# Reciprocals and norm pieces of a cross attention queued on VectorE behind the last instruction written in their step

## The chip, the cores and the metric

The kernel runs on one core of one Trainium2 chip: TensorE (PE), VectorE (DVE), ScalarE (ACT), GpSimd (POOL) and the DMA queues of SyncE (SP). The metric is the device time of one execution in microseconds (us), lower is better. Times are medians over several runs; the profile shows a single execution.

## The reference

One decoder layer in float32 on x of 16 sequences x 112 tokens x 512 features, with a context of 16 x 375 x 512: a self attention, a masked cross attention and a feed-forward block, each on a normalised x and each added to x. Of it the cross attention matters here:

```python
q = proj(hs, Wq, bq)            # 16 heads of 32
k, v = proj(at, Wk, bk), proj(at, Wv, bv)
scores = einsum('bhsd,bhtd->bhst', q, k) / sqrt(32)
scores = clip(where(attend, clip(scores, -50, 50), -10000), -50, 50)
probs = softmax(scores)
probs = probs / (probs.sum(-1) + 1e-8)
ctx = einsum('bhst,bhtd->bhsd', probs, v)
delta = clip(residual_scale, 0, 0.3) * (ctx @ Wo.T + bo)
delta = (delta - mean) / sqrt(var + 1e-5) * gamma + beta
x = x + delta                   # then layernorm(x) goes into the feed-forward block
```

## The kernel before

The program runs three stages: self attention (to about 330 us of the span), cross attention (to about 821 us) and the feed-forward block (to the end). The order of TensorE's instructions is the order in which the program is written, by hand. The other engines' orders are made by a scheduler when the kernel is built: among the instructions that its own clock holds ready for an engine it takes the one written first. Each engine then works through its queue in that order, whatever the chip's timing is.

**Steps.** The cross attention goes through 16 batches b and, in each, three thirds kc of the 375 context rows. `cross.step(b, kc, ...)` is one step, called (b,kc) here. In the timeline a step begins with the scores, TensorE's L929. It writes, in this order:

1. the scores of this third into two PSUM tiles "sc", and their exponentials on ScalarE (L1330) into tiles e or es;
2. for the third before: the weighted values (`weigh`, L940), the additions that sum its exponentials into the batch's es (`add`, VectorE, L1367; only for kc over 0), and at the end of a batch `divide`: the key sums on TensorE (L951), their copy into r on ScalarE (L1376), the copy of the unnormalised output into xyT (L1378), and a generator `quotients`, kept in `self.parts`;
3. the Relu check of the scores on ScalarE (L1338), which gives the score banks free;
4. `f.fill(us)`: filler work for TensorE, about us long, mostly keys and values of the next batch. Its products go into the three banks of the tag "mm" in turn, and VectorE reads each one out (the bank reads L907, L1019, L1023, L1035, L1076, L1078). Queries are read out by ScalarE (L892);
5. for b > 0 and kc > 0, pieces of `self.parts`.

`quotients` has four pieces, each a reciprocal of a quarter of r (L1383) and a product into xyT (L1384), and at its end a Relu on ScalarE (L1386). Two pieces are taken in the step with kc 1 and the rest with kc 2. As `divide` for batch b-1 is written in step (b,0), the pieces in (b,1) and (b,2) belong to batch b-1. Where b is a multiple of 4, step (b,0) takes all four at once and without any tie (L1346); the last batch's are taken after the loop.

**Norm pieces.** The main loop takes pieces of a generator `finish` in the steps with kc > 0 of batches that are not the first of their group of four: 3 in each step of an odd place in the group, 2 in an even one (L1818). At batch 1 they are the norm before the cross attention for the last group (`Norm.steps`: an rstd chain of 12 tiny instructions, L784 to L796, then one L802 for each of 4 tiles). At batches 5 and 9 they are `AfterCross.finish` for a whole group of tokens: one chain, then for each of 3 or 4 tiles two products and the statistics (L1291, L1299, L776, L777), then `Norm.steps` of the next norm.

**The ties.** Both kinds of piece stand in a `tc.issue_after(ins)`. It puts what is written inside it on the engine of `ins` (VectorE here) behind `ins` in that engine's queue: an order of issue, without a wait for the end of `ins`. ScalarE's instructions inside are not tied. Before, `ins` is `cross.last`, the addition L1367 that was written last. In a step with kc 1 no addition is written, so `cross.last` is there an addition of the step before. And an addition is written one step later than its exponentials, but its place in VectorE's queue is where these are ready, one step earlier:

```profile
494.22 1.14 PE L929 MATMUL sc<-q,kT 32*125 32x112 f32 x32
...
501.90 1.54 DVE L1383 RECIPROCAL r<-r 128x112 f32<-128x112 f32 x2
...
507.42 1.14 PE L929 MATMUL sc<-q,kT 32*125 32x112 f32 x32
...
518.13 1.14 PE L929 MATMUL sc<-q,kT 32*125 32x112 f32 x32
```

These are rows of the timeline (start, length, engine, line): steps (5,0), (5,1) and (5,2) begin at 494.22, 507.42 and 518.13. The two reciprocals at 501.90 are written in (5,1) and run in (5,0).

Of the kernel before, what the change touches and what calls it, by code (L numbers as in the profile page):

```python
# [584 lines left out]
def mixed(a, b, skip=0):  # L585

    a, b = iter(a), iter(b)
    for _ in range(skip):
        yield next(a)
    while True:  # L590
        took = [next(p, None) for p in (a, b)]
        if took[0] is None and took[1] is None:
            return
        yield sum(t for t in took if t is not None)
# [3 lines left out]
def finite_layer(  # L598
# [30 lines left out]
    nc = tc.nc  # L629
# [22 lines left out]
    def pair(name, tag="e", bufs=3):  # L652
        return evp.tile([P, 2, HG, S], F32, tag=tag, name=name, bufs=bufs)
# [267 lines left out]
    def scores(k_of, q_of, rows_):  # L921

        scs = [psum("sc", [P, 2, 512]) for _ in range(2)]
        views = [
            s[:rows_, :, : HG * S].rearrange("p i (j s) -> p i j s", j=HG) for s in scs
        ]
        for j in range(C):
            for i in range(HG):
                nc.tensor.matmul(  # L929
                    views[i // 2][:, i % 2, j, :], k_of(i, j), q_of(i, j), start=True, stop=True  # L930
                )
        return views
# [171 lines left out]
    def after_self(tiles, norm):  # L1104

        for t in tiles:
            yield from project(
                wo, t, lambda acc: nc.vector.tensor_tensor(xr[:, t, :], acc, xr[:, t, :], ALU.add)
            )
            stats(xr[:, t, :], norm.l, t)  # L1110

    class SelfAttention:
# [35 lines left out]
        def step(self, b, grp, f, us, prepared):  # L1148
            b, v, es = self.next
            if b + 1 < B:  # L1150
                self.begin(b + 1, grp)
            with tc.issue_after(self.behind.ins):
                for _ in range(prepared):
                    next(w2_prep, None)
            first = max(0.45 * us, min(us, 5.5))
            f.fill(first)
            eTs = []
            for e, share in zip(es, (0.45 * (us - first), 0.35 * (us - first))):
                tr = psum("sc", [P, 2, 512])
                trv = tr[:S, :, : HG * S].rearrange("p i (j s) -> p i j s", j=HG)  # L1160
                for i in range(2):
                    for j in range(C):
                        nc.tensor.transpose(trv[:, i, j, :], e[:, i, j, :], ident[:S, :S])  # L1163
                eT = pair("eT")
                nc.scalar.copy(eT[:S], trv)
                eTs.append(eT)
                f.fill(share)
            y = psum("ys", [P, C, S])
            weighted_values(y, v[b % GB][:S], eTs, True, True)
            nc.scalar.copy(xyT[:, :, ts(b, S)], y)  # L1170
            f.drain()
# [96 lines left out]
    class AfterCross:  # L1268
# [15 lines left out]
        def finish(self):  # L1284
# [23 lines left out]
                yield 0.0  # L1308
            yield from self.norm.steps()

    class Cross:


# [4 lines left out]
        def step(self, b, kc, q, keys, f, us):  # L1318
            scs = scores(
                lambda i, j: keys.third(keys.k[ds(i * DH, DH), j], kc),  # L1320
                lambda i, j: q[ds(i * DH, DH), j, ts(b % 2, S)],
                KP,
            )
            n = b * KC + kc
            late = self.late

            es = [(pair("es", "es", 3) if kc == 0 else pair("e"))[:KP] for _ in scs]
            self.late = (b, kc, keys.v[kc][:KP], es)
            for i, sc in enumerate(scs):
                nc.scalar.activation(  # L1330
                    es[i], sc, AF.Exp, scale=scl[:, n : n + 1], bias=bia[:, n : n + 1]
                )
            self.weigh(late)
            for i in range(2):
                self.add(late, i)
            self.divide(late)
            for i, sc in enumerate(scs):
                nc.scalar.activation(  # L1338
                    sc,
                    sc,  # L1340
                    AF.Relu,
                    scale=nscl[:, n : n + 1],
                    bias=limit[:KP, :1],
                    accum_out=low[:KP, 2 * n + i : 2 * n + i + 1],
                )
            if kc == 0 and b % GB == 0:  # L1346
                for _ in self.parts:
                    pass
            f.fill(us)
            if b > 0 and kc > 0:  # L1350
                with tc.issue_after(self.last):
                    for _ in range(2 if kc == 1 else C):
                        next(self.parts, None)

# [49 lines left out]
    def load_blocks(u, i):  # L1404

        o = block_tile("f")
        for half in range(2):
            nc.sync.dma_start(
                out=o[:, ds(2 * half, 2)].rearrange("p s k m -> p (s k) m"),
                in_=f_w[i][:, ts(u + UNITS * half, P)].rearrange("(c p) m -> p c m", p=P),  # L1410
            )
        behind = tc.issue_after(done[-2]) if len(done) > 1 else nullcontext()
        with behind:
            s_sums(o[:, 4:], *(o[:, k] for k in range(4)))
        return o
# [359 lines left out]
    cross = Cross()  # L1775
# [3 lines left out]
    for b in range(B):  # L1779
        g, bl = divmod(b, GB)  # L1780
        us = 0.0
        if b + 2 < B:
            kv.append(Keys(b + 2))
        if b + 1 < B:
            kv[b + 1].sums()
            us += 19.5
        if bl == 0:
            if g == 0:
                f.add(after_self(whole[3], n2[3]))
                finish = n2[3].steps()  # L1790
            elif g < 3:
                c = AfterCross(whole[g - 1], n3[g - 1])
                f.add(c.projections())
                finish = c.finish()
            us += 13.0 if g < 3 else 0.0
        if b + 1 < B:


            f.add(kv[b + 1].pieces())
            if b % 2:  # L1800
                queries = qs[(b + 1) // 2].pieces()
                us += 6.0
                if bl == 3 and g < 3:
                    n = n2[3] if g == 0 else n3[g - 1]
                    queries = mixed(queries, n.transposes(), 6)
                    us += 2.0
                f.add(queries)
        if b == B - 1:
            after = [AfterCross(whole[g], n3[g]) for g in (2, 3)]
            f.add(after[0].projections())  # L1810
            us += 10.5
        if b == B - 2:
            ready.update({(0, i): load_blocks(0, i) for i in range(2)})
        if b == B - 1:
            passes[0].token_sums()
        for kc in range(KC):
            cross.step(b, kc, qs[b // 2].q, kv[b], f, us / KC)
            if bl > 0 and kc > 0:  # L1818
                with tc.issue_after(cross.last):
                    for _ in range(2 + bl % 2):  # L1820
                        next(finish, None)
        f.drain()
# [100 lines left out]
@with_exitstack  # L1923
def decoder_layer(ctx: ExitStack, tc: tile.TileContext, *args):
    nc = tc.nc
    flag = ctx.enter_context(tc.tile_pool(name="flag", bufs=1))
    unfit = flag.tile([1, 1], I32, name="unfit")
    finite_layer(tc, unfit, *args)
    with tc.If(nc.values_load(unfit, min_val=0, max_val=1, skip_runtime_bounds_check_because="a comparison gives 0 or 1") > 0):
        general_layer(tc, *args)  # L1930
# [49 lines left out]
```

## Time and profile before

| | us |
|---|---|
| median of 3 runs (lowest, highest) | 1359.68 (1359.52, 1360.47) |
| the profiled execution | 1361.94 |
| its span, first to last instruction | 1360.2 |
| mean granted TensorE clock | 0.998 of full speed |
| TensorE busy in the span | 1338.4 (98%) |
| TensorE busy, 345 to 830 us | 482.29 of 485.00 |
| VectorE busy, 345 to 830 us | 327.19 of 485.00 |
| ScalarE busy, 345 to 830 us | 245.16 of 485.00 |
| L1383, reciprocals, 64 of them | 51.4 busy, 0.829 each |
| L1367, additions, 64 of them | 68.9 busy, 1.088 each |

How to read the profile: times are from the start of the span. A row of the timeline has the start, the length, the engine, the line of the kernel, the operation, out<-in with shapes and the number of instructions merged into it; in brackets stands how long the engine stood idle before it and whom it waited for. TensorE's float32 matmuls show as two records each, so x8 is four matmuls. Matmuls are pipelined and the ends of their records are modelled: the spacing of starts tells more than the lengths. A row of the table of windows has a stretch, its length, then the busy time of PE, PEld (weight loads), DVE, ACT and POOL with the number of instructions, the granted clock, the share of the DMA engines and GB/s.

### The profile page before, as it was taken

The page shows a single profiled execution, that of the slowest core. Times are in us where ns is not written, and L with a number is a line of the kernel's source. Part 1 is how long each engine was busy: PE and PEld are TensorE (multiplying, and loading weights), DVE is VectorE, ACT ScalarE, POOL GpSimd, SP SyncE. Part 2 cuts the span into 40 slices and gives each one's busy share as a digit, 9 for nine tenths or more (in the row PEclk, how much of TensorE's full clock was granted, in tenths as well). Part 3 has the DMA queues.
Part 4 walks back from the last instruction along what each step waited for, and adds up shares of the span by engine and source line. Part 5 has one row for each costly group of instructions (what it writes and reads, how often), then busy time and mean ns, then how long its engine had stood idle before and what let it go on. Part 6 is the DMA issues. An engine that isn't in the chain of part 4 may idle for free.

```text
span 1360.2 us, 20765 instructions
## 1 busy us (share of the span) xinstructions
PE 1338.4 (98%) x8508; PEld 840.2 (62%) x8508; DVE 820.0 (60%) x1666; ACT 476.9 (35%) x933; POOL 47.4 (3%) x72
## 2 busy tenths in 40 slices
PE   8999999999999999999999999999999999999997
PEld 5555555556788778868887874544555555555553
DVE  3267987873666577657765588557653245554332
ACT  2445664554445535454545553201110011111000
POOL 3000001040000100000000000000000000000000
PEclk9999999999999999999999999999999999999999
DMA  9100003711111111111121111111031112322201
GB/s 312 62 1 0 32 1 94 245 37 40 27 28 28 35 28 28 28 28 27 37 45 28 32 48 31 47 47 47 33 123 62 47 62 70 93 83 72 93 0 57
DMA packets 93579, 76.16 MB, mean 56 GB/s; under 512 B 44657, under 2 KB 81568, under 8 KB 91172
## 3 DMA queue, kind: packets, MB, share of 16 engines
q1 hardware_dynamic: 91744, 71.51, 17.3%
q0 software_dynamic: 736, 1.65, 0.4%
q8 instruction: 69, 1.13, 0.4%
q10 hardware_dynamic: 996, 1.59, 0.3%
q14 instruction: 34, 0.28, 0.1%
HBM read 63.72 MB, written 11.01 MB: 55 GB/s over the span
## 4 chain that ended last, share of the span: by engine, by line
PE 92%; DVE 5%; ACT 1%; issue 1%; DMA 1%; POOL 0%; DVEq 0%; ACTq 0%; POOLq 0%
PE gate L1547 12%; PE mm L884 10%; PE mm L1013 9%; PE mm L902 8%; PE ys L1547 7%; PE mm L913 7%; PE mm L1073 6%; PE gate L1481 6%; PE mm L1547 5%; PE sc L929 5%; PE ys L940 4%; PE ys L1481 4%; PE mm L1481 3%; PE sc L1163 2%; PE mm L845 1%; PE mm L951 1%
## 5 line engine op out<-in xcount | busy, mean ns | idle before, releaser
L1330 ACT ACTIVATE e<-sc,bia,scl 125x896 f32<-125x896 f32 x64 | 68.5, 1095 | 133.9 <-PE sc L929 133.9
L1338 ACT ACTIVATE sc<-sc,limit,nscl 125x896 f32<-125x896 f32 x96 | 103.2, 1075 | 0.0
L1367 DVE TENSOR_TENSOR es<-es,e 125x896 f32<-125x896 f32 x64 | 68.9, 1088 | 55.7 <-ACT e L1330 55.6
L1547 PE MATMUL gate<-t,f 128*128 128x448 f32 x256 | 101.4, 539 | 0.0
L1481 PE MATMUL gate<-h,f 128*128 128x448 f32 x224 | 86.6, 539 | 0.0
L1547 PE MATMUL gate<-xyT,f 128*128 128x448 f32 x192 | 80.1, 540 | 0.0
L1130 ACT ACTIVATE e<-sc,mx 112x112 f32<-112x112 f32 x256 | 64.6, 400 | 41.1 <-DVE mx L1126 41.1
L1383 DVE RECIPROCAL r<-r 128x112 f32<-128x112 f32 x64 | 51.4, 829 | 45.3 <-ACT r L1376 45.2
L1547 PEld LDWEIGHTS gate<-t,f 128*128 128x128 f32 x256 | 48.6, 190 | 47.6 <-issue 47.2
L1547 PE MATMUL ys<-t,f 128*128 128x448 f32 x192 | 77.4, 539 | 0.0
L1563 ACT COPY u<-gate 128x448 f32<-128x448 f32 x16 | 8.5, 532 | 183.5 <-PE gate L1547 110.5
L1481 PEld LDWEIGHTS gate<-h,f 128*128 128x128 f32 x224 | 42.5, 190 | 41.3 <-issue 40.9
L902 PE MATMUL mm<-xv,cT 128*125 128x512 f32 x144 | 66.3, 602 | 0.0
L1013 PE MATMUL mm<-kt,xks 128*128 128x188 f32 x360 | 65.1, 324 | 0.0
L1013 PEld LDWEIGHTS mm<-kt,xks 128*128 128x128 f32 x360 | 59.7, 190 | 2.9 <-issue 0.7
L1547 PEld LDWEIGHTS ys<-t,f 128*128 128x128 f32 x192 | 36.5, 190 | 35.7 <-issue 35.5
L902 PE MATMUL mm<-wv,xyT 128*112 128x512 f32 x128 | 58.0, 596 | 0.0
L1125 DVE TENSOR_REDUCE mx<-sc 112x8 f32<-112x896 f32 x32 | 33.5, 1084 | 40.6 <-PE sc L929 40.5
L1493 DVE TENSOR_TENSOR h<-h,h 128x896 f32<-128x896 f32 x32 | 32.8, 1085 | 40.9 <-PE ys L1481 31.7
L1547 PEld LDWEIGHTS gate<-xyT,f 128*128 128x128 f32 x192 | 36.0, 190 | 34.4 <-issue 33.0
L929 PEld LDWEIGHTS sc<-q,kT 32*125 32x125 f32 x1536 | 46.2, 183 | 15.3 <-issue 14.5
L929 PE MATMUL sc<-q,kT 32*125 32x112 f32 x1536 | 54.7, 279 | 0.0
(222 smaller groups left out, 2435.8 us busy)
## 6 DMA issues: line engine op xcount, KB each, us to landing
f<-in_f_w SPq DMA_DIRECT2D x64, 256.0 KB, 3.2
f<-blocks SPq DMA_DIRECT2D x14, 1024.0 KB, 4.8
cT<-in_ctx SPq DMA_DIRECT2D x32, 250.0 KB, 3.9
w<-in_f_w SPq DMA_DIRECT2D x4, 1024.0 KB, 10.3
blocks<-w SPq DMA_DIRECT2D x4, 1024.0 KB, 5.7
cT<-in_ctx SPq DMA_DIRECT2D x32, 126.0 KB, 3.5
xr<-in_x SPq DMA_DIRECT2D x2, 1024.0 KB, 10.7
out_y<-o SPq DMA_DIRECT2D x8, 256.0 KB, 3.2
```

The costliest lines, as they stand in the source:

```text
L884: nc.tensor.matmul(acc[:, :n], w[:, c, ts(j, P)], src[:, c, :], start=(c == 0), stop=(c == C - 1))
L902: nc.tensor.matmul(acc[:n, :], src[:, c, :], w[:, c, :], start=(c == 0), stop=(c == C - 1))
L913: nc.tensor.matmul(acc, xyT[:, c, ts(t, P)], w[:, c, :], start=(c == 0), stop=(c == C - 1))
L929: nc.tensor.matmul(views[i // 2][:, i % 2, j, :], k_of(i, j), q_of(i, j), start=True, stop=True)
L1013: nc.tensor.matmul(acc[:, m], w[:, k, ts(m, P)], x[:, k], start=k == 0, stop=k == 1)
L1073: nc.tensor.matmul(acc, x[:, k, :n], w[:, k], start=k == 0, stop=k == 1)
L1130: nc.scalar.activation(e[:, i, j, :], sc[:, i, j, :], AF.Exp, scale=SCALE, bias=mx[:, i, j : j + 1],)
L1330: nc.scalar.activation(es[i], sc, AF.Exp, scale=scl[:, n : n + 1], bias=bia[:, n : n + 1])
L1338: nc.scalar.activation(sc, sc, AF.Relu, scale=nscl[:, n : n + 1], bias=limit[:KP, :1], accum_out=low[:KP, 2 * n + i : 2 * n + i + 1],)
L1367: self.last = nc.vector.tensor_tensor(total, total, late[3][i][:KP], ALU.add).ins
L1481: nc.tensor.matmul(banks[m][bank], o[:, c, ts(m, P)], t[:, c, :], start=first and c == 0, stop=c == UNITS - 1, skip_group_check=True,)
L1547: nc.tensor.matmul(bank, o[:, s, k, :], t[:, k, :], start=first and k == 0, stop=k == 1, skip_group_check=True,)
```

## The change

A function `latest()` returns the VectorE instruction written last so far. Both ties now take it in place of `cross.last`. For the pieces of `self.parts` that is the last VectorE instruction of the step's filler, where the step has written any; for the norm pieces, which are taken after the step's call, it is the last product of `quotients` where the step has written one, else the same. What is computed, the instructions, and TensorE's order stay as they are.

```diff
+    def latest():
+
+        return next(
+            i
+            for i in reversed(nc.cur_bb.bb.instructions)
+            if i.engine == mybir.EngineType.DVE
+        )
+
     class Cross:
...
             f.fill(us)
             if b > 0 and kc > 0:
-                with tc.issue_after(self.last):
+                with tc.issue_after(latest()):
                     for _ in range(2 if kc == 1 else C):
                         next(self.parts, None)
...
         for kc in range(KC):
             cross.step(b, kc, qs[b // 2].q, kv[b], f, us / KC)
             if bl > 0 and kc > 0:
-                with tc.issue_after(cross.last):
+                with tc.issue_after(latest()):
                     for _ in range(2 + bl % 2):
                         next(finish, None)
```

## The prediction

> **What bounds the kernel now.** I read the page first, then who TensorE waited for in the cross attention (345 to 830 us), then the timeline around the longest of those waits, then the busy time of single steps. The page:
>
> ```profile
> PE 1338.4 (98%) x8508; PEld 840.2 (62%) x8508; DVE 820.0 (60%) x1666; ACT 476.9 (35%) x933; POOL 47.4 (3%) x72
> ...
> L1383 DVE RECIPROCAL r<-r 128x112 f32<-128x112 f32 x64 | 51.4, 829 | 45.3 <-ACT r L1376 45.2
> ```
>
> TensorE sets the time; VectorE matters only where TensorE has to wait for it. The reciprocals stand at the head of VectorE's queue for 45.2 us waiting for ScalarE's copy of the key sums, with the bank reads behind them. What that costs TensorE (line waited for: us, times, longest):
>
> ```profile
> PE mm L1073 <- DVE v L907: 2.4, 2, 1.4
> PE mm L884 <- DVE kT L1023: 0.3, 1, 0.3
> ```
>
> So there is little to win. By the starts of successive matmuls against their usual spacing the losses are 1.6 us at 502.5, 0.45 at 524.3 and 1.15 at 725.6: 3.2 in all, 0.24% of the run. The first, in the timeline (start, length, engine, line):
>
> ```profile
> 498.88 0.54 ACT L1376 COPY r<-mm 128x448 f32<-128x448 f32 x1
> ...
> 499.37 1.41 DVE L1299 SCALAR_TENSOR_TENSOR xr<-d,rstd,xr 128x512 f32<-128x512 f32 x2
> ...
> 501.34 1.44 PE L1013 MATMUL mm<-cT,xk 128*128 128x188 f32 x8
> 501.90 1.54 DVE L1383 RECIPROCAL r<-r 128x112 f32<-128x112 f32 x2
> ...
> 503.49 0.68 DVE L907 COPY v<-mm 125x512 f32<-125x512 f32 x1
> ...
> 504.22 1.13 PE L1073 MATMUL mm<-xv,cT 128*125 128x256 f32 x4 [1.44 <-DVE v L907]
> ```
>
> This is step (5,0) (batch 5, first third). Norm pieces and a pair of reciprocals, written for (5,1), run a step early, ahead of the first bank read L907. The bank is due when L1013 ends, at 502.6; the read ends at 504.1. That is the pattern by which I price the rest: the mm tile has three banks, so the read of one is due two products later.
>
> **What moves.** Now the pieces may start after an addition that VectorE did one step before; after the change, only behind the last VectorE instruction written in their own step, in practice a bank read. Nothing is added or removed: 48 of the 64 reciprocals move (batches 4, 8, 12 and the last finish theirs on a path the diff leaves alone), with all norm pieces. No DMA and no SP or POOL instruction is among them; the closing Relu (L1386, ScalarE) isn't tied but follows the last product. The durations, from one start to the next:
> - a pair of reciprocals with products: 806.93 to 808.72, 1.8 us;
> - one rstd chain: 520.40 to 523.72 less the addition inside, 2.3;
> - one tile of after-cross norm (L1291, L1299, statistics): 0.66 + 1.72 = 2.4, two interleaved 4.1;
> - two L802: 1.0.
>
> **Part 1, the gain.** (5,0) loses norm and reciprocals, so L907 is on time: -1.6. The 1.15 at 725.6 is batch 11's four reciprocals in (12,0), on the untouched path: it stays. At 524.3 L1023 will still have norm work before it: 0 (bounds -0.45 to +0.45).
>
> **Part 2, plain pairs.** Most steps get 1.8 us after their last bank read. TensorE then runs scores (1.14), weighted values (0.97) and two products before it needs a bank; the first bank read comes some 3.5 us after the scores began and can slip by two products less its own length, 1.27 + 0.86 - 0.5 = 1.6. Hidden, 0. If that cover went, each would cost up to 1.8.
>
> **Part 3, norm bursts.** Behind the last bank read of (5,1) now stand a pair, the chain and two tiles: 1.8 + 2.3 + 4.1 = 8.2; of (5,2) a pair, a tile, a chain, one L802: 1.8 + 2.4 + 2.3 + 0.5 = 7.0. For batch 9: 8.2, then a pair, two tiles and a chain, again 8.2. They land in steps with this much busy time (length; PE, PEld, DVE, ...):
>
> ```profile
> 518.13:528.19 10.06, 9.77 (x106) 8.87 (x105) 9.52 (x27) 5.48 (x9) 1.14 (x1) 1.00 0.40 92
> 528.19:537.54 9.35, 9.35 (x97) 6.07 (x96) 4.18 (x10) 5.56 (x9) 0.00 (x0) 1.00 0.01 2
> 648.61:658.15 9.54, 9.54 (x106) 8.86 (x105) 9.16 (x27) 5.48 (x9) 1.21 (x1) 1.00 0.42 96
> 658.15:667.50 9.35, 9.35 (x97) 6.08 (x96) 5.94 (x14) 5.56 (x9) 0.00 (x0) 1.00 0.01 3
> ```
>
> Step (5,2): of 9.5 VectorE us, 5.6 were norm work that leaves (1.7 of a tile, a chain, three L802); 3.9 + 8.2 = 12.1 in 10.06, so 2.0 spill into (6,0). There L907 is due by 536.6 (L1013 at 535.31 plus 1.27). If the spill and the whole second burst stand before it, it ends at 528.2 + 2.0 + 7.0 + 0.7 = 537.9: 1.3 late. If VectorE's order lets it in between the links of the chain, as bank reads were at 620 to 626, it costs 0. I take 0.7. Step (9,2): 6.8 leave (649.15 to 653.66 without an addition 3.5, a chain, two L802); 9.2 - 6.8 + 8.2 = 10.6 in 9.54, 1.1 spill; in (10,0) L907 is due at 666.5, and with 1.1 + 8.2, the key sums' differences (2.1 at 658.54) and itself it ends at 670.2: 3.7 late at worst, 0 at best. I take 2.0. Batch 1 has only 5.1 us (a pair, a chain, two L802) and 2.8 of such work; VectorE's free time there is 3.7 us in 389.51 to 399.01 and 5.8 in the step after: 0.
>
> **Part 4, additions pushed back.** The additions that the key sums need are written one step later than the pair, and of the work that is ready VectorE's queue has the earlier written first, as here the differences L1443. In (14,2), which also holds four token differences, the second addition was already last:
>
> ```profile
> 800.92 1.08 DVE L1443 TENSOR_TENSOR t<-xyT,t 128x896 f32<-128x896 f32 x1
> ...
> 801.92 0.72 DVE L1023 SCALAR_TENSOR_TENSOR kT<-mm,dbk,kT 128x188 f32<-128x188 f32 x2
> 802.57 1.08 DVE L1367 TENSOR_TENSOR es<-es,e 125x896 f32<-125x896 f32 x1
> ...
> 803.56 1.09 PE L951 MATMUL mm<-es,ones 125*32 125x448 f32 x8
> ```
>
> Its exponential was ready at 798.3, yet it ran at 802.57, and the key sums L951 (1.09, elsewhere 0.94) barely got it. VectorE has no free time in this step. It now gets a pair at its start (behind (14,1)) and one behind L1023, both ahead of that addition: 1.8 to 3.6 late; 0 if the order lets the addition in first. I take 2.7, nearer the order seen. (10,2) gets a pair and two L802 more and may hold back (11,0)'s key sums: 0 to 2.8, taken 0.5.
>
> **The sum.** -1.6 + 0 + 0 + 0.7 + 2.0 + 2.7 + 0.5 = +4.3 us. The profiled execution took 1361.94 us, its span 1360.2 with 1.7 around it, so it would become 1366.2. The median of the runs shown, 1359.68, is 2.26 below that execution; the same shift gives 1364.0, 0.32% slower.
>
> [...]
>
> **Rivals.**
> - A, no change (the other side): one mechanism, the place in VectorE's queue. If in (6,0), (10,0) and (15,0) the bank reads and the addition slip in before the moved work, only part 1 is left: 1359.68 - 1.6 = 1358.1. It decides once parts 3 and 4 come to under about 4.3 us. For it: reads were let in between chain links in step (9,0). Against: L907 was not, in (5,0), nor the addition in (14,2).
> - B, faster: the work behind the bank reads removes all three losses, and nothing new appears: 1359.68 - 3.2 = 1356.5. Against: 725.6 is on the untouched path, and 518 to 528 gets busier.
> - C, much slower: every upper bound at once, -1.6 + 1.3 + 3.7 + 3.6 + 2.8 = +9.8, 1369.5. The closing Relu adds to it: with its read it takes 0.67 + 0.2 us and now falls into the first third of the batch after next, between the exponentials. The step at 801.70 is 6.51 long and its score banks come free at 6.29, so 0.7 more could show there.
> - That the edit does nothing (the last instruction is the same addition where a step wrote no bank read): counted with A.
>
> **How the numbers follow.** Forecast 0.54, A 0.29, B 0.08, C 0.09. Runs here differ by 0.07%, and about 0.2% (2.7 us) is what can be told from no change. Faster: B, 0.08. Same: A, 0.29. Slower: forecast and C, 0.63. The range runs from a little below A, 1357.9, to C, 1369.5; the forecast's own is 1362 to 1368.
>
> **What would show it.** In the profile after: no TensorE wait for L907 near 502; VectorE's wait at L1383 for r down from 45.2 us to about 17.5 (5.5 at 463.5, 5.6 at 592.2, 6.5 at 722.6, the path left alone); in the other batches the reciprocals after the last bank read of their step. New TensorE waits for L907 in (6,0) and (10,0), and for the addition L1367 before L951 in (15,0). If these are missing, A is right and parts 3 and 4 fall; if TensorE waits at every step for bank reads behind a pair, part 2's cover was wrong.

## The result and the profile after

The changed kernel takes 1376.06 us (median; 1372.80 to 1376.58) against 1359.68 (1359.08 to 1360.47) on the same chip: 1.0114 times as long, 95% interval 1.0103 to 1.0125. A second set gave 1375.77 against 1359.31, 1.0116 (1.0101 to 1.0132). The forecast was 1364.0 with a range to 1369.5: right that it gets slower, 12 us short in the size. The profiled execution took 1375.94 us with a span of 1374.2, 14.0 more than the span before.

The page of the changed kernel (every line number behind the new function is 8 higher: L1367 is now L1375, L1383 is L1391, L1386 is L1394):

```profile
PE 1343.0 (98%) x8508; PEld 839.7 (61%) x8508; DVE 820.5 (60%) x1666; ACT 475.1 (35%) x933; POOL 43.0 (3%) x72
...
L1391 DVE RECIPROCAL r<-r 128x112 f32<-128x112 f32 x64 | 50.3, 822 | 22.1 <-ACT r L1384 22.1
```

Every engine runs as many instructions as before. VectorE's wait at the reciprocals fell from 45.3 to 22.1 us (forecast: about 17.5), as the edit is built to do, and the program got longer all the same. Whom TensorE waited for between 345 and 845 us, after (line waited for: us, times, longest):

```profile
PE mm L951 <- DVE es L1375: 5.7, 3, 3.1
PE mm L884 <- ACT q L892: 3.5, 3, 1.2
PE mm L1073 <- DVE v L907: 1.0, 1, 1.0
PE mm L884 <- DVE kT L1023: 0.7, 1, 0.7
PE mm L1013 <- DVE v L1078: 0.5, 1, 0.5
PE mm L1073 <- DVE kT L1019: 0.3, 1, 0.3
```

Before it was 2.7 in two rows. The two longest rows are new, and only one of them concerns VectorE: the key sums L951 wait for an addition, and the query products L884 wait for ScalarE. The 1.0 for L907 is the old loss in (12,0); no other step waits for L907.

**Where the 14 us are.** The ends of matmul records are modelled, so the idle time in brackets shows a part of each loss only (3.14 of 4.07 us in (10,0) below). The length of a step, from the start of its scores L929 to the next step's, holds all of it. Step lengths of the changed kernel less those of the kernel before, in the profiled executions (an empty last column: no wait of that step is listed above):

| step | us | TensorE waits there for |
|---|---|---|
| (5,0) | -1.70 | nothing any more (before: L907) |
| (5,2), (15,2) | -0.44, -0.42 | |
| (3,2), (7,2), (11,2) | +1.43 each | ScalarE's query read L892 |
| (3,0), (7,0), (11,0) | +0.36 each | |
| (6,0), (10,0), (15,0) | +2.07, +4.07, +2.20 | the addition L1375, at the key sums |
| (14,2) | +1.37 | bank reads L1019 and L1078 |
| (1,2) | +0.95 | bank read L1023 |
| (6,2), (10,2), (9,2) | +0.16, +0.16, +0.07 | |
| all | +13.8 | |

The cross attention went from 491.9 to 505.7 us. It began at 329.6 and 329.8, and what follows it took 538.7 and 538.6. So the question is not whether time was lost elsewhere, but why two waits arose that the prediction did not price.

**The wait for ScalarE.** Step (3,2) of the changed kernel, timeline:

```profile
449.86 1.14 PE L929 MATMUL sc<-q,kT 32*125 32x112 f32 x32
...
452.09 0.39 DVE L1392 TENSOR_TENSOR xyT<-xyT,r 128x112 f32<-128x112 f32 x2
...
452.52 0.67 ACT L1394 ACTIVATE r<-r,limit 128x448 f32<-128x448 f32 x1 [8.10 <-DVE xyT L1392]
...
453.19 2.07 ACT L1338 ACTIVATE e<-sc,bia,scl 125x896 f32<-125x896 f32 x2
...
457.30 1.13 ACT L892 ACTIVATE q<-mm,bq 128x224 f32<-128x224 f32 x3
...
457.80 1.02 PE L884 MATMUL mm<-xyT,xq 128*128 128x224 f32 x4 [1.16 <-ACT q L892]
```

The closing Relu L1394 needs the batch's last product L1392. It stands in ScalarE's queue ahead of this step's exponentials L1338, because that is where it was written. Now that the products come a step later, ScalarE stands idle for 8.10 us at it, and the exponentials start 3.33 us after the scores; before, they started 1.18 after. All behind them moves by as much: the query read comes 7.44 us into the step, before it was 5.31, and TensorE waits for the bank. The same step before, in which the Relu runs ahead of the scores:

```profile
447.81 0.67 ACT L1386 ACTIVATE r<-r,limit 128x448 f32<-128x448 f32 x1 [4.96 <-DVE xyT L1384]
...
448.29 1.14 PE L929 MATMUL sc<-q,kT 32*125 32x112 f32 x32
...
449.47 1.10 ACT L1330 ACTIVATE e<-sc,bia,scl 125x896 f32<-125x896 f32 x1 [0.89 <-PE sc L929]
...
453.60 0.80 ACT L892 ACTIVATE q<-mm,bq 128x224 f32<-128x224 f32 x2
```

Every odd batch has query products in its filler; the wait shows in the last steps of batches 3, 7 and 11.

**The wait for the addition.** Step (10,0) of the changed kernel, timeline:

```profile
661.92 0.74 DVE L1291 SCALAR_TENSOR_TENSOR d<-d,seen,gamma 128x512 f32<-128x512 f32 x1
...
663.08 1.14 PE L929 MATMUL sc<-q,kT 32*125 32x112 f32 x32
...
664.94 0.92 PE L951 MATMUL mm<-es,ones 125*32 125x448 f32 x4
...
667.15 0.73 DVE L1299 SCALAR_TENSOR_TENSOR xr<-d,rstd,xr 128x512 f32<-128x512 f32 x1
...
667.89 1.06 DVE L1375 TENSOR_TENSOR es<-es,e 125x896 f32<-125x896 f32 x1
...
669.00 0.95 PE L951 MATMUL mm<-es,ones 125*32 125x448 f32 x4 [3.14 <-DVE es L1375]
```

VectorE is busy for 14.90 of the 15.00 us from 655 to 670 and waits for no other engine. Ahead of the addition at 667.89 stand a pair of reciprocals with their products (659.79 to 661.78) and norm pieces (661.92 to 667.8), 2.0 and 5.9 us. The two halves of the key sums start 4.06 us apart, and no bank read is waited for. Before, the key sums of this step ran in one go, with about 0.5 us between the starts of the halves:

```profile
660.01 0.94 PE L951 MATMUL mm<-es,ones 125*32 125x448 f32 x8
```

### The profile page after: what moved, and what is told of

It reads as the page before. It is cut to its first block, busy times and chain, and to the rows that moved or that the text cites. A ratio compares the mean times of both kernels' runs of the same rounds, so it can differ in the third digit from the quotient of the medians.

```text
span 1374.2 us, 20789 instructions
## 1 busy us (share of the span) xinstructions
PE 1343.0 (98%) x8508; PEld 839.7 (61%) x8508; DVE 820.5 (60%) x1666; ACT 475.1 (35%) x933; POOL 43.0 (3%) x72
## 3 DMA queue, kind: packets, MB, share of 16 engines
q0 software_dynamic: 736, 1.65, 0.4%
## 4 chain that ended last, share of the span: by engine, by line
PE 87%; DVE 8%; ACT 3%; DMA 1%; issue 1%; POOL 0%; ACTq 0%; POOLq 0%
PE gate L1555 12%; PE mm L1013 9%; PE mm L884 8%; PE mm L902 7%; PE ys L1555 7%; PE mm L913 7%; PE gate L1489 6%; PE mm L1073 6%; PE mm L1555 5%; PE sc L929 4%; PE ys L1489 4%; PE ys L940 3%; PE mm L1489 3%; DVE r L1391 2%; PE sc L1163 2%; PE mm L845 1%
## 5 line engine op out<-in xcount | busy, mean ns | idle before, releaser
L1338 ACT ACTIVATE e<-sc,bia,scl 125x896 f32<-125x896 f32 x64 | 68.1, 1093 | 161.2 <-PE sc L929 161.2
L1346 ACT ACTIVATE sc<-sc,limit,nscl 125x896 f32<-125x896 f32 x96 | 103.1, 1074 | 0.0
L1375 DVE TENSOR_TENSOR es<-es,e 125x896 f32<-125x896 f32 x64 | 68.5, 1086 | 45.0 <-ACT e L1338 45.0
L1391 DVE RECIPROCAL r<-r 128x112 f32<-128x112 f32 x64 | 50.3, 822 | 22.1 <-ACT r L1384 22.1
L884 PE MATMUL mm<-xyT,xq 128*128 128x224 f32 x256 | 51.9, 357 | 4.2 <-ACT q L892 3.5
L929 PEld LDWEIGHTS sc<-q,kT 32*125 32x125 f32 x1536 | 46.2, 183 | 15.3 <-issue 14.5
```

Of the source, the lines that this page charges most:

```text
L884: nc.tensor.matmul(acc[:, :n], w[:, c, ts(j, P)], src[:, c, :], start=(c == 0), stop=(c == C - 1))
L929: nc.tensor.matmul(views[i // 2][:, i % 2, j, :], k_of(i, j), q_of(i, j), start=True, stop=True)
L1338: nc.scalar.activation(es[i], sc, AF.Exp, scale=scl[:, n : n + 1], bias=bia[:, n : n + 1])
L1346: nc.scalar.activation(sc, sc, AF.Relu, scale=nscl[:, n : n + 1], bias=limit[:KP, :1], accum_out=low[:KP, 2 * n + i : 2 * n + i + 1],)
L1375: self.last = nc.vector.tensor_tensor(total, total, late[3][i][:KP], ALU.add).ins
L1391: nc.vector.reciprocal(r[:, c], r[:, c])
```

## The experiments

The theory (T) after this reading: what a moved piece costs is what stands behind it in two queues, ScalarE's behind the closing Relu, VectorE's additions behind pieces that the scheduler now lets in first. The rival (R): VectorE has no room for the work in the steps where it now falls, and bank reads pay, whatever the order. Diffs are against the changed kernel for e1 to e5, against the kernel before for e6 to e8, and against e7 for e9.

**e1: the reciprocals' tie alone.**

```diff
-                with tc.issue_after(latest()):
+                with tc.issue_after(cross.last):
                     for _ in range(2 + bl % 2):
                         next(finish, None)
```

> The reciprocals behind the last VectorE instruction of their step, the norm pieces tied as before. Theory T (what moved holds up two queues: ScalarE's, behind the closing Relu that waits for the last product, and VectorE's additions, behind which the key sums wait): the waits of queries on ScalarE, 0.95 at batch 1 and 1.42 each at batches 3, 7, 11 (5.2 us), and those of (14,2) and (15,0) (3.6) are all there without a norm piece: about +7 to +9 us against before, some 1367. Rival R (VectorE is over-full where the norm bursts fall, and its order hardly matters): the reciprocals alone cost under 3 us, under 1363.

Measured: 1367.28 us, ratio 1.0051 (1.0034 to 1.0067), cross attention +6.65 us. The query waits are there in full ((3,2), (7,2), (11,2) +1.43, (3,0), (7,0), (11,0) +0.36), and so are (14,2) +1.37 and (15,0) +2.20. (5,0) gains 1.40. (6,0) and (10,0) are unchanged, and so is (1,2): the 0.95 that T expected at batch 1 is not there.

**e2: the norm pieces' tie alone.** They are tied behind the last instruction of the filler, the reciprocals where they were.

```diff
             f.fill(us)
+            self.cut = latest()
             if b > 0 and kc > 0:
-                with tc.issue_after(latest()):
+                with tc.issue_after(self.last):
...
-                with tc.issue_after(latest()):
+                with tc.issue_after(cross.cut):
                     for _ in range(2 + bl % 2):
```

> The norm pieces behind the last VectorE instruction that the filler of their step wrote, the reciprocals tied as before. T: only the key sums of (6,0) and (10,0) wait, less than with the pairs (2.1 and 4.1 us there), and (5,0) loses part of its 1.7 us wait: +1 to +4 us, some 1362. R: nearly the whole of the 15 us, over 1370.

Measured: ratio 1.0011 (1.0001 to 1.0020), cross attention +0.75 us: (10,0) +1.47, (9,2) +0.72, (5,2) +0.20, (6,0) +0.09, and -1.70 in (5,0). That is at the lower edge of what was expected. The two halves of the edit come to 6.65 + 0.75 = 7.4, but together to 13.8. The difference lies in (6,0) and (10,0), 6.14 together against 1.56 in the halves, in (5,0), whose gain each half has (1.40 and 1.70) and the whole only once, and in smaller steps ((1,2) +0.95, against 0). In (10,0) the timeline suggests the reason: of the 7.9 us ahead of the late addition, the pair's 2.0 alone cost nothing (e1) and the norm pieces alone 1.47 (e2, with 0.5 us of listed wait for the addition), while both cost 4.07.

**e3: the closing Relu left out.** The kernel then leaves out the check of r by the accumulator `top`; all else is the changed kernel.

```diff
-            nc.scalar.activation(
-                r, r, AF.Relu, scale=-1.0, bias=limit[:, 1:], accum_out=top[:, b : b + 1]
-            )
```

> The changed kernel without the closing Relu of each batch (the range check of the key sums is left out, nothing else reads it). T: TensorE's waits for queries from ScalarE at batches 1, 3, 7, 11 go, 5 us of the 15, some 1371; the key sums' waits stay. R: the Relu is 0.7 us on an engine that is busy a third of the time: no more than 1 us.

Measured: 1371.42 us, ratio 1.0082 (1.0065 to 1.0098). All six steps of the ScalarE rows are back to 0.00, which is 3 x 1.43 + 3 x 0.36 = 5.4 us. (6,0), (14,2) and (15,0) are as in the changed kernel, and so the Relu has no part in what they lose here.

**e4: the additions put first.** Each step writes its own additions behind its exponentials and ahead of the pieces, and the two after the loop go.

```diff
             self.weigh(late)
-            for i in range(2):
-                self.add(late, i)
             self.divide(late)
+            for i in range(2):
+                self.add(self.late, i)
```

> The changed kernel with the additions written in the step of their own exponentials, ahead of the moved pieces of that step, and so ahead of them in VectorE's choice. T: the key sums' waits in (6,0), (10,0), (15,0), 8.3 us, mostly go; a wait for bank read L907 of up to 1.3 and 3.7 us may take their place in the first two: 1367 to 1371. R: the same work stands in the same steps, so under 2 us come back.

Measured: 1368.15 us, ratio 1.0056 (1.0039 to 1.0073). The waits at the key sums are gone, (15,0) is -0.15. What takes their place in e4, TensorE's waits:

```profile
PE mm L1073 <- DVE v L907: 3.3, 3, 1.7
PE sc L929 <- ACT q L892: 1.5, 3, 0.5
PE sc L929 <- ACT sc L1346: 1.2, 1, 1.2
```

Apart from the 1.0 in (12,0), the bank read L907 is now late in (6,0) and (10,0). These steps are +1.73 and +2.88, but not all of it is L907. In both, and in (2,0), the scores L929 stand still half way for ScalarE's query read L892, which now stands behind the closing Relu (second row). (2,0) has only this wait, and is +0.88. That leaves about 0.85 and 2.0 for L907.

The query waits of (3,2), (7,2) and (11,2) are gone, since a pair behind an addition comes behind that step's exponentials, and so does the Relu that waits for it. The Relu still costs, at other places: the three times 0.88, the 0.36 in each of (3,0), (7,0) and (11,0), which stays, and (15,1), which is +1.63. There the scores wait for the score check L1346 (third row), ahead of which the Relu stands. In the changed kernel ScalarE is idle for 0.90 us at the Relu in (15,0), and the longer wait for the addition covers that. This is read from the timeline; no run has e4 without the Relu.

**e5: the closing Relu with all its work, written one step later.** They are collected and issued in the next step with kc 0, behind ScalarE's last instruction.

```diff
-            nc.scalar.activation(
-                r, r, AF.Relu, scale=-1.0, bias=limit[:, 1:], accum_out=top[:, b : b + 1]
-            )
+            self.closing.append((b, r))
...
+            if kc == 0:
+                with tc.issue_after(latest(mybir.EngineType.Activation)):
+                    self.close()
```

> The changed kernel with each closing Relu written one step group later, behind the score checks of the next batch's first third on ScalarE; all the work is there. T (the Relu costs by its place in ScalarE's queue, not by its 0.9 us): the waits for queries at batches 3, 7, 11 and the 0.36 us before them go as without the Relu, 5.4 us: cross attention about 500 us, some 1370 in all. R (it costs as work): no change from the changed kernel's 505.8 us there.

Measured: 1368.42 us, ratio 1.0063 (1.0047 to 1.0078). The same six steps are at 0.00 with all of the Relu's work present. So the 5.4 us are the price of its place in ScalarE's queue, not of its work, 0.67 us and a read of 0.2.

**The changed kernel again**, beside e4 to e6:

> The changed kernel once more, as a control. T and R: cross attention 505.8 us as before within 0.2, every step as in the first profile; in all 1374 to 1376, where differences of 2 us come from the clock in the first 20 us and not from the change.

Measured: 1375.77 us, and every step within 0.02 us of the first profile but one: (10,0), +7.09 in place of +4.07. In e3 and e5 it is +6.88 and +5.72. The wait there is the same 3.1 us in all four. What differs is TensorE's granted clock, the third column from the right in these windows (stretch, length; busy PE, PEld, DVE, ACT, POOL; clock, DMA share, GB/s); first the repeat, then e5:

```profile
666.00:667.00 1.00, 0.00 (x0) 0.00 (x0) 1.00 (x3) 0.04 (x1) 0.00 (x0) 0.80 0.00 0
667.00:668.00 1.00, 0.81 (x4) 0.19 (x4) 1.00 (x3) 0.00 (x0) 0.00 (x0) 0.50 0.02 8
...
673.00:674.00 1.00, 1.00 (x3) 0.46 (x2) 0.00 (x0) 0.00 (x0) 0.00 (x0) 0.79 0.00 0
```

```profile
664.00:665.00 1.00, 0.20 (x2) 0.14 (x4) 1.00 (x2) 0.00 (x0) 0.00 (x0) 0.95 0.00 0
665.00:666.00 1.00, 1.00 (x4) 0.00 (x0) 1.00 (x4) 0.00 (x0) 0.00 (x0) 0.50 0.02 8
...
668.00:669.00 1.00, 1.00 (x3) 0.42 (x2) 0.83 (x6) 0.76 (x3) 0.00 (x0) 0.84 0.00 0
```

The rows left out show 0.50 as well. If the clock was either full or half, a row of 0.80 had half clock for 0.40 us of its 1.00; by this estimate the repeat ran at half speed for 0.40 + 6 + 0.42 = 6.82 us, e5 for 0.10 + 3 + 0.32 = 3.42. In the first profile of the changed kernel the clock was 1.00 throughout this stretch. The cost against +4.07 is 3.02 us in the repeat, 2.81 in e3 and 1.65 in e5.

**e6: the kernel before, with the pieces of a kc 1 step tied behind the value read L907 that was written one step earlier, with kc 0.** Those of kc 2 stay behind the addition. `behind` returns the marked read in a kc 1 step, else `self.last`; both ties use it.

```diff
-                yield next(last)
+                took = next(last)
+                mark[self.b] = latest()
+                yield took
...
-                with tc.issue_after(self.last):
+                with tc.issue_after(self.behind(b, kc)):
...
-                with tc.issue_after(cross.last):
+                with tc.issue_after(cross.behind(b, kc)):
```

> The kernel before, with the pieces written in the steps with kc 1 (reciprocals and norm) tied behind the read L907 of the step before, and not behind an addition; those of kc 2 as before. T (the order against this one read made the wait of 1.7 us in (5,0), and the other steps have room): 1.7 us less than before in (5,0), nothing new elsewhere, cross attention 490.2 us. R (any push of this work makes new waits): a new wait of about the same size in (5,1) or (5,2), no gain.

Measured: 1361.86 us, ratio 1.0013 (1.0004 to 1.0023): a miss. (5,0) gains its 1.70, but (5,1) +1.32, (9,1) +1.34 and (9,2) +1.03 give back more. Here R is right: work put between L907 and the reads behind it makes these late (TensorE's longest waits are 0.8 us for L1023 and 0.5 for L1078; before, 0.3 and none).

**e7: e6, and batch 11's reciprocals not taken at once in (12,0).**

```diff
-            if kc == 0 and b % GB == 0:
+            if kc == 0 and b % GB == 0 and b < B - GB:
```

> As the last, and the reciprocals of batch 11, which no projection reads in step (12,0), are taken in (12,1) and (12,2) like those of an ordinary batch. T: also the 1.15 us in (12,0) go: cross attention 489 us, 2.9 less than before, some 1357. R: they make a wait of that size in (12,1) or (12,2).

Measured: 1361.37 us, ratio 1.0015 (1.0006 to 1.0024). (12,0) is 1.25 us shorter and nothing new appears, while (5,1), (9,1) and (9,2) cost as in e6. The steps of the profile come to +0.73 us, the medians to +2.06 (interval 0.8 to 3.3); why they differ is open.

**e8: the kernel before with only that condition.**

> The kernel before with one condition added: at (12,0) the four reciprocals of batch 11 are not taken at once but left to (12,1) and (12,2), tied behind the last addition as all others are. Theory T (a piece costs what it holds up in its queue, and at (12,0) nothing of the burst was needed there): the wait at (12,0) goes, step (12,0) is 1.25 us shorter as in the run before this one, all other steps stay within 0.15; cross attention 490.7 us against 491.9, ratio about 0.999. Rival R (VectorE has no room, moved work is given back later): (12,1), (12,2) or (13,0) longer by as much as (12,0) gains; cross attention 491.9.

Measured: 1358.28 us against 1359.93, ratio 0.9989 (0.9980 to 0.9998); (12,0) -1.25, all other steps within 0.02 us. As T said.

**e9: e7 with the norm pieces left behind the addition.** Only the reciprocals of kc 1 steps stand behind L907.

```diff
-                with tc.issue_after(cross.behind(b, kc)):
+                with tc.issue_after(cross.last):
                     for _ in range(2 + bl % 2):
                         next(finish, None)
```

> The kernel of e8, and the reciprocals of a batch's second step (kc = 1) tied behind the value read L907 of that step; the norm pieces stay behind the last addition. Theory T: (5,0) gains 1.4 as in e1_recip_only, since its reciprocals no longer stand ahead of a bank read, and the lone pairs are short enough (2 x 1.3 us) to delay nothing in (5,1), (9,1), (9,2): cross attention 489.3 us, ratio about 0.998. Rival R (any VectorE work put between L907 and the key copies L1023 delays these, so pairs alone are enough): (5,1) and (9,1) are longer by up to 1.3 each, as in e6, and the sum is 490.7 to 492.

Measured: 1357.60 us against 1359.93, ratio 0.9986 (0.9977 to 0.9995); (5,0) -1.00, less than the 1.4 expected, (12,0) -1.25, nothing given back. What is left of TensorE's waits in its cross attention:

```profile
PE mm L884 <- DVE kT L1023: 0.3, 1, 0.3
```

From e7 to e9 only the place of the norm pieces differs, and the cross attention goes from 492.65 to 489.66 us: in e6 and e7 it was the norm pieces that were too long to stand between two bank reads; a pair of reciprocals fits. This version is faster than both kernels, by 0.14% against the one before.

## Why the prediction was wrong in size

**The gain (part 1) was right.** (5,0) measured -1.70 for -1.6, the loss at 725.6 stayed until e8 removed its cause. 524.3 gave 0.44, the edge of the bounds stated.

**"Hidden, 0" for the plain pairs (part 2) was the main fault.** The step asked only which VectorE bank read comes behind a pair. It did not ask who else waits for the pair's product. The closing Relu does, at the head of ScalarE's in-order queue with the exponentials and the query reads behind it: 5.4 us, shown by e3 (taken away) and e5 (moved). The Relu was in the prediction, under rival C, but as 0.67 + 0.2 us of work "between the exponentials" that could show at the step from 801.70. It cost nothing there in the changed kernel ((15,0) is +2.20 with it and +2.19 without), where the wait for the addition covers it; in e4, without that wait, score banks are late at this place and (15,1) loses 1.63. It cost 1.43 in each of three other steps, which rival C did not name. That ScalarE reads the queries out (L892) stands in the description of the kernel, and was priced nowhere. (1,2) adds 0.95 where 0 was said for batch 1; it needs both ties, as neither e1 nor e2 has it.

**Norm bursts (part 3): the right steps, the wrong instruction, under half the size.** 0.7 + 2.0 was taken for (6,0) and (10,0); measured 2.07 + 4.07, both above the upper bounds of 1.3 and 3.7. The prediction looked for the bank read L907 as the victim. The addition ahead of the key sums is due earlier in the step and stands behind the burst as well; TensorE stops for it first, and by then L907 is in time. e4 shows both: with the additions first, their wait goes and L907 takes it up with about 0.85 and 2.0, close to the 0.7 and 2.0 forecast. So the price of the bank read holds in e4, and the step that failed was to take this read for the first instruction to be late. Of the signs named, the waits for L907 in (6,0) and (10,0) are absent, and the wait for the addition in (15,0) is there. The reason that part 4 gives for (15,0), an addition written later than the pieces, holds at (6,0) and (10,0) in the same way and was not carried over to them.

**Additions pushed back (part 4): right mechanism, a fair size.** (15,0) measured 2.20 for 2.7, at the place and by the wait foretold. (14,2) adds 1.37 for late bank reads, which had no price: its VectorE, said to have no free time, is given a pair more (805.35 to 807.1); the second pair, at 815.28, falls into (15,0). (11,0) was given 0.5; it has no wait for an addition, and its 0.36 is the Relu's.

**The clock.** The forecast's sum has no term for the granted clock. In (10,0), at twice its predicted size, the clock fell to 0.50 in three of four profiles with this wait, and they lost 1.65 to 3.02 us more than the fourth. That fits the distance between the 13.8 us of steps and the 16.4 us between the medians; the other executions have no profile, only a mean clock. In the first set the one run at a mean clock of 0.999 took 1372.80, while those at 0.996 took 1376.06 to 1376.58. So of the 12.1 us by which the forecast fell short, about 9.5 are in steps (13.8 against 4.3), and the other 2.6 are the clock's by my estimate from these means and profiles.

**Rival A** would have needed reads and additions slipped in ahead of the moved work; that order did not arise. The sum, by its own terms: gains 1.70 + 0.86, losses 5.37 (ScalarE), 8.34 (additions), 2.32 (bank reads) and 0.39, together +13.9 (the table's 13.8 within rounding).

**Still open.** Why the losses of (6,0) and (10,0) need both ties is read from one step's timeline and from e1 and e2; no run varies the length of the burst by itself. Why (1,2) needs both is not known.

## What to carry to other kernels

Before a piece of work is moved later, list every instruction that reads its result, on all engines, and walk down each reader's queue: in an in-order queue the price of a late operand is paid by whatever stands behind its reader, here 5.4 us behind a Relu of 0.67. Where several consumers share a stage, the one due first pays, so price the earliest due time, and price two moved bursts together, since each may fit alone (in (10,0) 0 and 1.47 us alone, 4.07 together). The gain came from one wait traced to one piece of code (e8, -0.11%), while the rule laid over all steps cost 1.14%.

## What the runs showed of the hardware

With the stop of TensorE in (10,0), 3.1 us by its records, the granted clock fell to 0.50 in three of four profiles (the repeat, e3, e5). In the fourth, the first profile of the changed kernel, it stayed at 1.00, and the repeat has the same order of instructions. The lengths at half clock, estimated as above from the rows, are 3.42 us in e5, 6.82 in the repeat and 6.84 in e3 (0.74, six rows of 0.50, 0.84): two of them are twice the third. What sets these lengths is not shown. In the repeat TensorE resumed at 667.19, 0.6 us after the clock had fallen by this estimate; in e5 it resumed at 664.8, 0.1 us before.

The self attention is the same in every run. In the first profiles of the two kernels it has a stop of TensorE of 2.2 us, which ends at 146.5 us before and 146.8 after, and the clock is 1.00 from 140 to 155 us in both profiles. In e3 (first) and e5 (second) it was lower from 145 to 150:

```profile
145.00:150.00 5.00, 5.00 (x16) 3.04 (x15) 5.00 (x11) 3.87 (x11) 0.00 (x0) 0.69 0.00 2
```

```profile
145.00:150.00 5.00, 5.00 (x15) 2.77 (x16) 5.00 (x11) 4.15 (x12) 0.00 (x0) 0.66 0.01 2
```

By the same estimate that is 0.62 x 5 = 3.1 and 0.68 x 5 = 3.4 us at half clock, in a stretch in which TensorE is busy for all of the 5.00 us. The rows don't show whether the stop brought the clock down.

The profiled execution of the kernel before has a stretch at half clock in its first 25 us, seen in its windows:

```profile
15.00:20.00 5.00, 3.27 (x17) 2.00 (x16) 1.96 (x4) 2.40 (x5) 2.22 (x6) 0.89 1.05 388
20.00:25.00 5.00, 5.00 (x11) 2.34 (x10) 4.44 (x20) 0.53 (x1) 0.00 (x0) 0.77 1.05 387
```

That is, estimated in the same way, 0.22 x 5 + 0.46 x 5 = 3.4 us at half speed (the clock is 0.50 from 19 to 22 us); in e8 and e9 the same rows show 1.00, and step (0,2) starts at 352.73 (e9) instead of 354.45. These 1.7 us are probably most of the 2.26 us by which the profiled execution of the kernel before was above its median, which the prediction had carried along unexplained; the executions of the median have no profile. The first profile of the changed kernel has the same stretch (0.90 and 0.76 in these rows); its repeat, with all steps up to there alike, starts (10,0) at 661.27 instead of 663.08.
